# Six-layer stack: the inverse norms of a sequence move from VectorE to GpSimd

## The chip, the cores and the metric

One NeuronCore of a Trainium2 chip runs the whole program. Its engines, as the profile names them, are PE (TensorE, matmuls, with its weight loads as PEld), DVE (VectorE), ACT (ScalarE), POOL (GpSimd) and SP (SyncE, which only issues transfers here). The metric is the device time of one execution in microseconds, median of the runs shown, lower is better.

## The reference, cut to what matters

Four stages run one after the other on 16 sequences of 256 tokens of 128 features: a linear attention, a mixture of experts, a causal linear attention, and then a stack of six layers, each a local attention and a feed-forward. The stack takes most of the time, and the change lies in its attention:

```
qkv = x @ Wqkv;  q, k, v = split(qkv)            # 16 heads of 64
l2norm(t) = t / max(norm(t, axis=-1), 1e-12)
q = l2norm(q) * q_scale;  k = l2norm(k) * k_scale
q = q*cos*scale + rotate_half(q)*sin*scale        # k with 1/scale
out = softmax(mask(8 * q k^T over two windows of 32)) v
x = out @ Wo + x
x = feed_forward(layernorm(shifted x)) + x
```

The norms are those of 64 numbers each: for one sequence 2 tiles of 128 tokens, query and key, 16 heads, so 64 sums of squares in each of 128 partitions. Of each the kernel needs the inverse square root of max(sum, 1e-24).

## The kernel before, in words

A tile is 128 tokens. A sequence has two tiles (TPS), two sequences make a unit, and eight units go through each layer, so the stack has 96 sequences in all. For each of them the code makes a number of *steps*, each a short run of instructions on one engine.

For each tile and for query and key in turn, `projections` makes: on PE the product with the weights into a PSUM buffer "pair" (L1071, two matmuls of 512 columns); on ACT the squares of the product (`square`, L1092); on DVE the two rotary products, `first` (L1078, with the cosines, into a buffer "t1") and `second` (L1085, the swapped halves with the sines, into "t2"), and `squares` (L1098), which sums the squares of each head into "ss"; on POOL `rotated` (L1095), the sum t1 + t2.

When the four sums of a sequence are there, `rotations` makes the step `norms`, which calls `inv_norm`: on DVE one reduction of pairs (L1049, where the second entry of each pair in "ss" was filled with 1e-24 once, so that the reduction is the clamp), a first guess made from the bits of the number with a tile "magic" (L1050), and three Newton rounds of three instructions (L1054, L1055, L1056). These eleven instructions work on 128 x 64 elements. Then `turned` makes, four times in a sequence: on POOL `scale` (L1141), which multiplies t1 by the inverse norms; on PE eight transposes (L1145); on ACT a copy to "qT" or "kT" (L1151).

The rest of a sequence: `windows` (PE L1196, ACT L1187 and L1202); `attention` for each tile with scores (PE L1228), the mask and the maximum (DVE L1236, L1250), the subtraction (POOL L1253), exp (ACT L1257), the total and its reciprocal (DVE L1261, L1262), the division (POOL L1265), transposes (PE L1269), a copy (ACT L1310), the mix with the values (PE L1280) and a copy (ACT L1289); `output` (PE L1340, 32 matmuls, DVE L1349). For each unit a feed-forward follows (PE L1366, L242, L1401, L1421; DVE, ACT, and on POOL a variance's root, L1381 and L221).

The order of the work is set while the program is built, by the class `Plan`. It plays the steps through with an assumed duration for each (the number behind the engine's name in `step(...)`), takes on each engine the ready step of lowest rank for which the buffers are free, and writes the instructions in that order. A rank is the tile's number, plus an entry of the dictionary `due`, plus an entry of the dictionary given to `Plan`, which is looked up by the names of the enclosing function and of the step's function. A lower rank is taken earlier. On the chip each engine then runs its instructions in that fixed order and waits by semaphores for what other engines give it. The buffers that tie the steps together are few: four "pair", five "t1" (a sequence holds four of them, from the product until the transposes have read them), three "ss", two "t2", two "e". `norms` is a DVE step of assumed duration 4.4, `scale` a POOL step of 1.87, `rotated` one of 2.32.

Of the kernel before, what the change touches and what calls it, by code (L numbers as in the profile page):

```python
# [9 lines left out]
F32 = mybir.dt.float32  # L10
I32 = mybir.dt.int32
AF = mybir.ActivationFunctionType
ALU = mybir.AluOpType
AX = mybir.AxisListType
PSUM = bass.MemoryType.PSUM

P = 128
NSEQ = 16
SEQ = 256
TPS = SEQ // P  # L20
# [5 lines left out]
HEADS = 16  # L26
# [37 lines left out]
class Plan:  # L64
# [14 lines left out]
    def step(self, eng, work, fn, after=(), takes=(), uses=(), rank=0, table=None, count=0):  # L79
        after = [a for a in after if a is not None]  # L80
        kind = getattr(fn, "func", fn).__qualname__.split(".<locals>.")[-2:]
        rank += self.due.get(".".join(kind), 0)
        s = Step(eng, work, fn, after, takes, uses, rank, table, count)
        self.steps.append(s)
        return s
# [107 lines left out]
def tile_kernel(ctx: ExitStack, tc: tile.TileContext, a: dict, out: bass.AP):  # L193
    nc = tc.nc
    pe, act, dve, pool, sp = nc.tensor, nc.scalar, nc.vector, nc.gpsimd, nc.sync
# [145 lines left out]
    with ExitStack() as st:  # L341
# [5 lines left out]
        def several(pl, n, shape, name):  # L347
            return [pl.tile(shape, F32, name=f"{name}{k}", tag=f"{name}{k}") for k in range(n)]

        slots = {  # L350
            "bank": several(pa, 6, [P, 512], "pb"),
            "two": several(pa, 1, [P, 2, 512], "pw"),
            "xin": several(wa, 2, [P, TPU, P], "a_xin"),
            "a": several(wa, 8, [P, 512], "a_b"),
            "h": several(wa, 4, [P, 384], "b_h"),
            "x": several(wa, 5, [P, 512], "bc_x"),
            "e": several(wa, 4, [P, 8, 2, DH], "c_e"),
            "va": several(wa, 3, [P, TPS, 8, DH + 1], "c_va"),
# [29 lines left out]
        due = {  # L388
            "linear": -12, "experts": -5, "causal": 0, "hidden": 0, "outer": 0, "values": 0,
            "product": -1, "ends": -1, "turn": 0, "scores": 0, "diagonal": -1, "weigh": 0,  # L390
            "ratio": -1, "y": 0, "join": 0,
        }
        step = plan.step
# [587 lines left out]
    with ExitStack() as st:  # L981
        wps = [wp, st.enter_context(tc.tile_pool(name="wp2", bufs=1))]
        wps = [wp, st.enter_context(tc.tile_pool(name="wp2", bufs=1))]
        cd = st.enter_context(tc.tile_pool(name="cd", bufs=1))
        sd = st.enter_context(tc.tile_pool(name="sd", bufs=3))
        pp = st.enter_context(tc.tile_pool(name="pp", bufs=1, space=PSUM))

        def several(pl, n, shape, name):
# [7 lines left out]
            "xw": several(cd, 2, [P, TPS * NB, P], "d_xw"),  # L996
            "sq": several(cd, 2, hs, "d_sq"),
            "t1": several(cd, 5, hs, "d_t1"),
            "ss": several(cd, 3, [P, 2, 2, HEADS, 2], "d_ss"),
            "t2": several(cd, 2, hs, "d_t2"),  # L1000
            "e": several(cd, 2, [P, 8, 2, 2 * WIN], "d_e"),
            "eT": several(cd, 2, [P, 8, P], "d_eT"),
# [4 lines left out]
        }  # L1007
        for kT in slots["kT"]:
            pool.memset(kT[:, :, 0:WIN], 0.0)
        for ss in slots["ss"]:  # L1010

            pool.memset(ss, 1e-24)
        plan = Plan(slots, {
            "projections.product": -3,
            "feed_forward.turn": 1.5,
            "attention.mix": -1.5,
            "attention.divide": -0.5,
            "output.product": 2,
            "attention.below": 5,
            "projections.first": -0.5,  # L1020
            "projections.squares": 0.5,
            "projections.second": -1,
            "final.turn_back": -3,
            "windows.turn": -1,
            "rotations.norms": 3,
        })

        due = {
# [4 lines left out]
        step = plan.step  # L1033

        def heads(ap):
            return ap.rearrange("p (h d) -> p h d", d=DH)
# [3 lines left out]
            return ap.rearrange("p (h x d) -> p h x d", x=2, d=DH // 2)[:, :, ::-1, :]  # L1040

        NN = TPS * 2 * HEADS
        magic = cd.tile([P, NN], I32, name="d_magic")
        pool.memset(magic, 1597463007)

        def inv_norm(ss):

            x, y, t = (sd.tile([P, NN], F32, name=f"d_n{k}", bufs=2) for k in "xyt")
            dve.tensor_reduce(x, ss.rearrange("p t g h b -> p (t g h) b"), AX.X, ALU.max)  # L1049
            dve.scalar_tensor_tensor(  # L1050
                y.bitcast(I32), x.bitcast(I32), -0.5, magic, ALU.mult, ALU.add
            )
            for _ in range(3):
                dve.scalar_tensor_tensor(t, y, 1.0, y, ALU.mult, ALU.mult)  # L1054
                dve.scalar_tensor_tensor(t, t, -0.5, x, ALU.mult, ALU.mult)  # L1055
                dve.scalar_tensor_tensor(y, t, 1.5, y, ALU.add, ALU.mult)  # L1056
            return y

        def projections(q, t):

            rank = q.rank + t
            xj = q.x[:, WIN + t * P : WIN + (t + 1) * P]
            o = Part()
            o.t1s, o.adds = [], []
            if t == 0:
                q.ss, q.reds = Buf("ss"), []

            def product(qk, pj):
                for hf in range(2):
                    c = qk * INNER + hf * 512  # L1070
                    pe.matmul(  # L1071
                        pj.t[:, hf * 512 : (hf + 1) * 512], lhsT=xj,
                        rhs=q.w["qkv"][:, c : c + 512], start=True, stop=True,
                    )

            def first(qk, pj, t1):
                cc = slice(qk * DH, (qk + 1) * DH)
                dve.tensor_tensor(  # L1078
                    t1.t, heads(pj.t), bc(q.lay.tab[:, 0, t, cc], hs, 1), ALU.mult
                )  # L1080

            def second(qk, pj, t2):
                cc = slice(qk * DH, (qk + 1) * DH)
                h4 = [P, HEADS, 2, DH // 2]
                dve.tensor_tensor(  # L1085
                    t2.t.rearrange("p h (x d) -> p h x d", x=2), swapped(pj.t),
                    bc(q.lay.tab[:, 1, t, cc].rearrange("p (x d) -> p x d", x=2), h4, 1),
                    ALU.mult,
                )

            def square(pj, sq):
                act.activation(sq.t, heads(pj.t), AF.Square)  # L1092

            def rotated(t1, t2):
                pool.tensor_tensor(t1.t, t1.t, t2.t, ALU.add)  # L1095

            def squares(qk, sq):
                dve.tensor_reduce(q.ss.t[:, t, qk, :, 0], sq.t, AX.X, ALU.add)  # L1098

            for qk in range(2):  # L1100
                pj, sq, t1, t2 = Buf("pair"), Buf("sq"), Buf("t1"), Buf("t2")
                mm = step(
                    "pe", 1.82, partial(product, qk, pj), [*q.ready, *q.loaded, q.gate(t)],
                    [pj, t1], rank=rank + due["project"], count=8,
                )
                s = step(
                    "act", 0.92,
                    partial(square, pj, sq),
                    [mm], [sq], [pj], rank,
                )  # L1110
                a1 = step("dve", 1.13, partial(first, qk, pj, t1), [mm, q.tabbed], [], [pj, t1], rank)
                a2 = step(
                    "dve", 1.13, partial(second, qk, pj, t2), [mm, q.tabbed], [t2], [pj],
                    rank + due["second"],
                )
                new = [] if q.reds else [q.ss]
                q.reds.append(
                    step(
                        "dve", 1.13, partial(squares, qk, sq), [s, *q.reds], new,
                        [sq] if new else [sq, q.ss], rank + due["squares"],  # L1120
                    )
                )
                o.adds.append(
                    step(
                        "pool", 2.32,
                        partial(rotated, t1, t2),
                        [a1, a2], [], [t1, t2], rank,
                    )
                )
                o.t1s.append(t1)  # L1130
            q.tiles.append(o)

        def rotations(q):


            def norms():
                q.rn = inv_norm(q.ss.t)

            def scale(t, qk, t1):
                k = (2 * t + qk) * HEADS  # L1140
                pool.tensor_tensor(t1.t, t1.t, bc(q.rn[:, k : k + HEADS], hs, 2), ALU.mult)  # L1141

            def turn(t1, pz):
                for c in range(8):
                    pe.transpose(  # L1145
                        pz.t[:, c * P : (c + 1) * P],
                        t1.t[:, 2 * c : 2 * c + 2, :].rearrange("p h d -> p (h d)"), ident,
                    )

            def put(dst, off, pz):  # L1150
                act.copy(  # L1151
                    dst.t[:, :, off : off + P], pz.t.rearrange("p (c n) -> p c n", n=P)
                )

            nm = step("dve", 4.4, norms, q.reds, [], [q.ss], q.rank + due["norms"])
            q.kT = Buf("kT")
            for t in range(TPS):
                turned(q, t, nm, scale, turn, put)
# [318 lines left out]
        for i in range(DEPTH):  # L1477
# [22 lines left out]
            for u in range(NU):  # L1500
                adds = []
                for s in range(SPU):
                    q = Seq()
# [171 lines left out]
```

## Time and profile before

| what | value |
|---|---|
| runs shown | 4375.12, 4375.44, 4377.77 us; median 4375.44 |
| the profiled execution: time, span from first to last instruction | 4371.72 us, 4369.9 us |
| mean granted TensorE clock | 0.989 |
| DVE busy in the span | 3633.8 us (83%) |
| ACT busy in the span | 2674.8 us (61%) |
| POOL busy in the span | 2978.6 us (68%) |
| first and last Newton product on DVE (L1056) | 1116.7 and 4268.2 us from the start |

The first three stages fill the span up to about 1095 us; the stack follows. The table of groups of instructions gives, for each line of the code, engine and shape, the count, the busy time, the mean duration of one, the idle time of the engine just before these instructions, and what released it. The table of waits tells who waited for whom. The timeline lists an engine's instructions in order of time, neighbours of one kind merged ("x4"). A PE that is busy need not be at its peak, since the ends of matmuls are modelled. Durations on POOL are rougher than on DVE and ACT.

### The profile page before, as it was taken

How to read it: one execution, taken by the hardware profiler on the slowest of the kernel's cores; microseconds unless marked ns; L12 is line 12 of the kernel's file. 1: busy time of each engine (PE TensorE's matmuls, PEld its weight loads, DVE VectorE, ACT ScalarE, POOL GpSimd, SP SyncE). 2: the span in 40 equal slices, each digit the busy share in tenths (PEclk: the TensorE clock that was granted, in tenths of full speed). 3: DMA queues.
4: the chain of work that ended last, by engine and by line, in shares of the span. 5: the costliest groups of instructions: out<-in, count | busy, mean ns of one | idle time of the engine just before them, and what ended most of it. 6: DMA issues, size and time to landing. Idle time of an engine off the chain costs nothing. (4 is left out here: it accounts for less than half of the span.)

```text
span 4369.9 us, 106120 instructions
## 1 busy us (share of the span) xinstructions
PE 4191.8 (96%) x45648; PEld 2978.9 (68%) x45648; DVE 3633.8 (83%) x6064; ACT 2674.8 (61%) x3514; POOL 2978.6 (68%) x1717
## 2 busy tenths in 40 slices
PE   8999999998699999999999999999999999999998
PEld 6777877877466666666666666666666666666666
DVE  6888888877788888878888888888888878888895
ACT  6766767664466566566656656666665665665654
POOL 2655545555787777767777778777777777777773
PEclk9999999999899999999999999999999999999999
DMA  3000000000000000000000000000000000000000
GB/s 88 4 6 6 3 4 1 4 3 3 20 2 11 2 13 2 7 11 2 13 2 6 11 2 13 2 7 11 2 12 2 7 11 2 2 2 6 6 14 18
DMA packets 30834, 37.13 MB, mean 8 GB/s; under 512 B 5407, under 2 KB 24349, under 8 KB 29597
## 3 DMA queue, kind: packets, MB, share of 16 engines
q1 hardware_dynamic: 30364, 30.35, 2.3%
q8 instruction: 359, 5.88, 0.6%
q14 instruction: 111, 0.90, 0.1%
HBM read 26.15 MB, written 4.19 MB: 7 GB/s over the span
## 5 line engine op out<-in xcount | busy, mean ns | idle before, releaser
L1095 POOL TENSOR_TENSOR d_t<-d_t,d_t 128x1024 f32<-128x1024 f32 x384 | 906.3, 2366 | 301.7 <-DVE d_t L1078 230.7
L1141 POOL TENSOR_TENSOR d_t<-d_t,d_ny 128x1024 f32<-128x1024 f32 x384 | 718.8, 1902 | 242.3 <-DVE d_ny L1056 242.3
L1071 PE MATMUL pp<-d_wqkv,xs 128*128 128x512 f32 x1536 | 736.7, 605 | 6.5 <-ACT d_sq L1092 1.6
L1340 PE MATMUL pp<-d_zT,d_wvo 128*128 128x256 f32 x3072 | 687.5, 382 | 1.2 <-DVE d_t L1078 0.5
L1340 PEld LDWEIGHTS pp<-d_zT,d_wvo 128*128 128x128 f32 x3072 | 575.9, 190 | 85.0 <-ACT d_xw L1202 1.3
L1092 ACT ACTIVATE d_sq<-pp 128x1024 f32<-128x1024 f32 x384 | 393.4, 1024 | 313.8 <-PE pp L1071 174.4
L1085 DVE TENSOR_TENSOR d_t<-pp,d_tab 128x1024 f32<-128x1024 f32 x384 | 466.3, 1215 | 135.4 <-ACT d_sq L1092 94.5
L1265 POOL TENSOR_TENSOR d_e<-d_e,d_z 128x1024 f32<-128x1024 f32 x192 | 363.5, 1902 | 229.6 <-DVE d_z L1262 228.3
L1289 ACT COPY d_zT<-pp 128x1024 f32<-128x1024 f32 x384 | 384.1, 1016 | 192.6 <-PE pp L1280 190.3
L1078 DVE TENSOR_TENSOR d_t<-pp,d_tab 128x1024 f32<-128x1024 f32 x384 | 463.7, 1209 | 19.0 <-ACT d_sq L1092 19.0
L1228 PEld LDWEIGHTS pp<-d_kT,d_qT 64*32 64x32 f32 x24576 | 230.2, 106 | 352.9 <-issue 202.1
L1098 DVE TENSOR_REDUCE d_ss<-d_sq 128x16 f32<-128x1024 f32 x384 | 463.3, 1209 | 0.1
L1280 PE MATMUL pp<-d_eT,d_xw 64*128 64x256 f32 x3072 | 425.9, 402 | 21.7 <-DVE d_t L1078 12.7
L1145 PE MATMUL pp<-ident,d_t 128*128 128x128 f32 x3072 | 404.2, 278 | 35.5 <-POOL d_t L1141 24.0
L1071 PEld LDWEIGHTS pp<-d_wqkv,xs 128*128 128x128 f32 x1536 | 271.4, 191 | 241.5 <-issue 217.2
L1145 PEld LDWEIGHTS pp<-ident,d_t 128*128 128x128 f32 x3072 | 344.8, 142 | 104.6 <-issue 56.4
L1257 ACT ACTIVATE d_e<-d_e 128x1024 f32<-128x1024 f32 x192 | 202.8, 1057 | 317.4 <-POOL d_e L1253 312.7
L1228 PE MATMUL pp<-d_kT,d_qT 64*32 64x64 f32 x24576 | 348.7, 223 | 28.7 <-DVE d_t L1078 25.0
L1253 POOL TENSOR_TENSOR d_e<-d_e,d_m 128x1024 f32<-128x1024 f32 x192 | 363.7, 1903 | 16.7 <-DVE d_m L1250 16.7
L848 POOL TENSOR_TENSOR c_e<-c_e,c_sm 128x1024 f32<-128x1024 f32 x128 | 248.7, 1950 | 178.2 <-DVE c_sm L844 121.8
L1280 PEld LDWEIGHTS pp<-d_eT,d_xw 64*128 64x128 f32 x3072 | 270.7, 187 | 104.0 <-ACT d_eT L1310 28.3
L835 POOL TENSOR_TENSOR c_e<-c_mn,c_e 128x512 f32<-128x512 f32 x128 | 139.7, 1091 | 196.3 <-ACT c_e L825 95.7
(187 smaller groups left out, 8083.1 us busy)
## 6 DMA issues: line engine op xcount, KB each, us to landing
d_wqkv<-L_ffn_Wqkv SPq DMA_DIRECT2D x6, 1024.0 KB
d_t<-L_ffn_Wqkv SPq DMA_DIRECT2D x10, 256.0 KB
d_t<-L_ffn_Wo SPq DMA_DIRECT2D x10, 256.0 KB, 3.0
a_xin<-L_attn_x SPq DMA_DIRECT2D x8, 256.0 KB, 2.9
keep<-bc_x SPq DMA_DIRECT2D x8, 256.0 KB, 2.0
d_t<-keep SPq DMA_DIRECT2D x8, 256.0 KB, 3.0
out<-d_t SPq DMA_DIRECT2D x8, 256.0 KB, 2.4
d_w<-L_ffn_W SPq DMA_DIRECT2D x6, 341.0 KB
```

Source lines behind the costliest of these rows:

```text
L1071: pe.matmul(pj.t[:, hf * 512 : (hf + 1) * 512], lhsT=xj, rhs=q.w["qkv"][:, c : c + 512], start=True, stop=True,)
L1078: dve.tensor_tensor(t1.t, heads(pj.t), bc(q.lay.tab[:, 0, t, cc], hs, 1), ALU.mult)
L1085: dve.tensor_tensor(t2.t.rearrange("p h (x d) -> p h x d", x=2), swapped(pj.t), bc(q.lay.tab[:, 1, t, cc].rearrange("p (x d) -> p x d", x= ...
L1092: act.activation(sq.t, heads(pj.t), AF.Square)
L1095: pool.tensor_tensor(t1.t, t1.t, t2.t, ALU.add)
L1098: dve.tensor_reduce(q.ss.t[:, t, qk, :, 0], sq.t, AX.X, ALU.add)
L1141: pool.tensor_tensor(t1.t, t1.t, bc(q.rn[:, k : k + HEADS], hs, 2), ALU.mult)
L1145: pe.transpose(pz.t[:, c * P : (c + 1) * P], t1.t[:, 2 * c : 2 * c + 2, :].rearrange("p h d -> p (h d)"), ident,)
L1228: pe.matmul(pS.t[b * WIN : (b + 1) * WIN, s0 : s0 + 2 * WIN], lhsT=qT.t[r, c, b * WIN : (b + 1) * WIN], rhs=kT.t[r, c, k0 : k0 + 2 * WIN], ...
L1280: pe.matmul(pz.t[:, par * 512 : (par + 1) * 512].rearrange("p (c n) -> p c n", n=QB)[:, :, j * WIN : (j + 1) * WIN], lhsT=q.xw.t[r, t * NB ...
L1289: act.copy(q.zT.t[:, 2 * t + g, :, :].rearrange("p h n -> p (h n)"), pz.t)
L1340: pe.matmul(pr.t[:, :SEQ], lhsT=q.w["vo"][:, h, :], rhs=q.zT.t[:, :, h, :], start=(h == 0), stop=(h == HEADS - 1),)
```

## The change

`inv_norm` is written for POOL and called from a POOL step of assumed duration 2.8. It clamps the sums in place, makes the first guess with the magic number as an immediate, and takes four instructions for a Newton round, since none of them has two tensors and a scalar. DVE keeps `squares`, which now writes a plain "ss". The fills of "ss" and the tile "magic" go, and two small buffers get three copies each in place of three buffers with two. The planner's second dictionary is rewritten: seven entries have other numbers, five are new.

```diff
-            "ss": several(cd, 3, [P, 2, 2, HEADS, 2], "d_ss"),
+            "ss": several(cd, 3, [P, TPS, 2, HEADS], "d_ss"),
...
-        for ss in slots["ss"]:
-
-            pool.memset(ss, 1e-24)
         plan = Plan(slots, {
-            "projections.product": -3,
+            "projections.product": -1,
             "feed_forward.turn": 1.5,
-            "attention.mix": -1.5,
+            "attention.mix": -4.5,
             "attention.divide": -0.5,
-            "output.product": 2,
-            "attention.below": 5,
-            "projections.first": -0.5,
-            "projections.squares": 0.5,
-            "projections.second": -1,
+            "output.product": 4,
+            "attention.below": 3,
+            "projections.first": -1.5,
+            "projections.squares": -1.0,
+            "projections.second": 3,
             "final.turn_back": -3,
             "windows.turn": -1,
             "rotations.norms": 3,
+            "join.turn": -3,
+            "join.turned_out": 4,
+            "rotations.turn": -0.5,
+            "attention.top": -1.5,
+            "rotations.put": -3,
         })
...
-        magic = cd.tile([P, NN], I32, name="d_magic")
-        pool.memset(magic, 1597463007)
-
-        def inv_norm(ss):
-
-            x, y, t = (sd.tile([P, NN], F32, name=f"d_n{k}", bufs=2) for k in "xyt")
-            dve.tensor_reduce(x, ss.rearrange("p t g h b -> p (t g h) b"), AX.X, ALU.max)
-            dve.scalar_tensor_tensor(
-                y.bitcast(I32), x.bitcast(I32), -0.5, magic, ALU.mult, ALU.add
+
+        def inv_norm(x):
+
+            y, t = (sd.tile([P, NN], F32, name=f"d_n{k}", bufs=3) for k in "yt")
+            pool.tensor_scalar(x, x, 1e-24, None, ALU.max)
+            pool.tensor_scalar(
+                y.bitcast(I32), x.bitcast(I32), -0.5, 1597463007.0, ALU.mult, ALU.add
             )
             for _ in range(3):
-                dve.scalar_tensor_tensor(t, y, 1.0, y, ALU.mult, ALU.mult)
-                dve.scalar_tensor_tensor(t, t, -0.5, x, ALU.mult, ALU.mult)
-                dve.scalar_tensor_tensor(y, t, 1.5, y, ALU.add, ALU.mult)
+                pool.tensor_tensor(t, y, y, ALU.mult)
+                pool.tensor_tensor(t, t, x, ALU.mult)
+                pool.tensor_scalar(t, t, -0.5, 1.5, ALU.mult, ALU.add)
+                pool.tensor_tensor(y, y, t, ALU.mult)
             return y
...
-                dve.tensor_reduce(q.ss.t[:, t, qk, :, 0], sq.t, AX.X, ALU.add)
+                dve.tensor_reduce(q.ss.t[:, t, qk, :], sq.t, AX.X, ALU.add)
...
-                q.rn = inv_norm(q.ss.t)
+                q.rn = inv_norm(q.ss.t.rearrange("p t g h -> p (t g h)"))
...
-            nm = step("dve", 4.4, norms, q.reds, [], [q.ss], q.rank + due["norms"])
+            nm = step("pool", 2.8, norms, q.reds, [], [q.ss], q.rank + due["norms"])
```

## The prediction

> **What bounds the kernel now.** I read the stack in equal windows first, then the waits of PE, then the timelines of one sequence. In the windows of the inner layers the columns are the stretch, its length, and the busy time with the count for PE, PEld, DVE, ACT and POOL, then the clock.
>
> ```profile
> 1500.00:2100.00 600.00, 591.84 (x7423) 401.51 (x7420) 513.78 (x752) 370.33 (x386) 454.84 (x239) 1.00 0.02 6
> 2100.00:2700.00 600.00, 592.12 (x7375) 400.35 (x7373) 513.56 (x751) 370.34 (x385) 455.20 (x239) 1.00 0.03 8
> ```
>
> PE is busy for 98.6% of such a stretch, DVE for 85.6%, POOL for 75.8%, at full clock. PE's ends are modelled, but the timeline below shows its runs set end to end with no gap, so PE's order sets the pace. PE does nothing less after the change: a gain can only come out of its idle time, or of shorter idle at the edges of layers.
>
> The groups of the steps in question, from the table of groups by shape (count | busy us, mean ns | idle before, releaser):
>
> ```profile
> L1141 POOL TENSOR_TENSOR d_t<-d_t,d_ny 128x1024 f32<-128x1024 f32 x384 | 718.8, 1902 | 242.3 <-DVE d_ny L1056 242.3
> ...
> L1050 DVE SCALAR_TENSOR_TENSOR d_ny<-d_nx,d_magic 128x64 int32<-128x64 int32 x96 | 104.1, 1085 | 3.3
> ...
> L1054 DVE SCALAR_TENSOR_TENSOR d_nt<-d_ny 128x64 f32<-128x64 f32 x288 | 72.2, 251 | 9.9
> ```
>
> POOL stands idle 242.3 us, 2.5 us a sequence, for DVE's inverse norms, and has nothing else to do then. L1050 takes 1085 ns where its like, L1056, takes 225: something holds it up. Now one sequence on POOL, on DVE and on PE (start, length, engine, line):
>
> ```profile
> 1625.45 1.90 POOL L1253 TENSOR_TENSOR d_e<-d_e,d_m 128x1024 f32<-128x1024 f32 x1
> 1629.85 7.48 POOL L1141 TENSOR_TENSOR d_t<-d_t,d_ny 128x1024 f32<-128x1024 f32 x4 [2.50 <-DVE d_ny L1056]
> 1637.30 1.89 POOL L1265 TENSOR_TENSOR d_e<-d_e,d_z 128x1024 f32<-128x1024 f32 x1
> ```
>
> ```profile
> 1624.03 1.21 DVE L1098 TENSOR_REDUCE d_ss<-d_sq 128x16 f32<-128x1024 f32 x1
> 1625.28 0.29 DVE L1049 TENSOR_REDUCE d_nx<-d_ss 128x64 f32<-128x128 f32 x1
> 1625.60 1.83 DVE L1050 SCALAR_TENSOR_TENSOR d_ny<-d_nx,d_magic 128x64 int32<-128x64 int32 x1
> ```
>
> ```profile
> 1633.13 0.45 PE L1228 MATMUL pp<-d_kT,d_qT 64*32 64x64 f32 x32
> 1633.51 1.99 PE L1145 MATMUL pp<-ident,d_t 128*128 128x128 f32 x16
> 1635.34 1.88 PE L1071 MATMUL pp<-d_wqkv,xs 128*128 128x512 f32 x4
> ```
>
> The last sum of squares ends at 1624.03 + 1.21 = 1625.24, the first scale (L1141) starts at 1629.85: 4.6 us. L1050 ends at 1627.43, just behind POOL's L1253 at 1627.35: it had waited for it. The first scale ends at 1631.7, and PE turns that tile at 1633.51, 1.8 us later; the second ends at 1633.6 and is turned at about 1634.4, **0.8 us** later. In the other sequence of the unit the scales start at 1663.33 and PE's first turn is at 1671.35, 6.1 us behind the first scale's end. So half of the sequences are tight.
>
> **What DVE loses.** L1049, L1050, L1054, L1055 and L1056: 27.3 + 104.1 + 72.2 + 64.9 + 64.9 = 333.4 us busy, with 2.8 + 3.3 + 3 x 9.9 = 35.8 us of gaps between them, 369 us in all, 3.85 us a sequence. DVE isn't the bound, so this counts only where PE waits for DVE. In the table of PE's waits the DVE rows of the stack are 25.0 (L1228), 12.7 (L1280), 6.0 (L1145), 5.3 (L1280) and 5.1 (L1269): 54 us is the most that a freer DVE can give. I take half, **-27 us**, because those waits sit behind products, not behind norms, and the order is new anyway. The 242 us of POOL's idle time are no gain by themselves: PE didn't wait there.
>
> **What POOL gains in work.** Fourteen instructions on 128 x 64, each using the one before it. No such row exists. The nearest are POOL's root, in the timeline:
>
> ```profile
> 1653.41 0.24 POOL L1381 TENSOR_SCALAR f_rs<-f_mv 128x4 f32<-128x4 f32 x1
> 1653.74 1.04 POOL L221 TENSOR_TENSOR f_rs<-f_rs,nhalf 128x4 f32<-128x4 f32 x1
> ```
>
> The second needs the first's result and starts 0.32 to 0.33 us after it: 0.24 of work and 0.085 of gap. Independent ones have no gap: four L1141 of 1.902 start 1.87 apart. For 64 elements in place of 4, the fills show the slope for one operand: 151 ns for 64 elements, 204 for 128, so 0.83 ns an element, and a scalar instruction takes 232 + 60 x 0.83 = 282 ns, 0.365 us with the gap. For two full tensors L1095 has 2366 ns at 1024 elements; with 232 fixed that is 2.08 ns an element, 365 ns at 64, 0.45 with the gap. Nine of these and five scalar ones: 9 x 0.45 + 5 x 0.365 = **5.9 us**. Lower end: all at the small row's 0.315, 4.4 us. Upper end: a fixed part of 352 ns, from the table rows L1463 (726 ns at 256) and L835 (1091 at 512), 7.0 us, and the integer guess as dear as L221's power adds 0.7: 7.7. I take 5.9, since the root is the nearest row in size and in dependence.
>
> Two rules bear on this. The Trainium skill, "Perfetto Trace Analysis", section GPSIMD Engine Instruction, says that spans of this engine are unreliable and that one should time from start to start. By spans alone the sum is 9 x 0.365 + 5 x 0.282 = 4.7; by starts, 5.9. The two rows above decide for starts, because the gap of 0.085 is visible. "GPSIMD Engine Reference", section Engine selection, speaks against the move: elementwise work belongs on VectorE, GpSimd being about twice as slow for two inputs. By it 14 x 2 x 0.225 = 6.3 us, an estimate that puts the step no cheaper than mine. The planner's 2.8 lies under all of these, even under the lower end.
>
> Per sequence (96 in 4268.2 - 1116.7 us, so 33.2 us each) POOL has 0.758 x 33.2 = 25.2 us of work. With 5.9 it has 31.1: 94% full.
>
> **What comes late.** With the old order POOL would start the norms at 1627.35, when L1253 is done, and the first scale at 1633.25 in place of 1629.85; in the other sequence the squares end at 1659.35, POOL is busy until 1660.83, and the scale starts at 1666.7 in place of 1663.33. Both are 3.4 us late. With the planner's 2.8 the same sum is 0.3. So the new order is made for scales that in truth arrive 3.1 us later. Behind the norms on POOL stand the four scales, then a division (L1265) or a subtraction (L1253): exp and the transposes of e come late too, with larger margins on PE. Where a turn has 0.8 us of margin in the plan, PE stands for 2.3 us, and every engine behind it.
>
> I assume that the new order has margins as the old one: one tight sequence in two. Of the 48 units the first and last of a layer run irregularly (joins, tables), so about 42 count: 42 x 2.3 = **+97 us**. In the fill at 1100 to 1200 us POOL is the late engine already (L1145 waits for L1141 three times, 24.0 us); there the norms take 5.9 for DVE's 4.0 us, **+6 us**.
>
> **The smaller edits**, together: fills of ss and magic (0.65 us before the stack, hidden by DVE's start) and the third copy of y and t, nothing; `squares` writes 16 numbers with a narrower stride, nothing. The new ranks move work that has the same length: DVE's second product now comes behind the first, the squares nearer to them, the mix earlier on PE, products and output later. No DMA is added. The order can be worth anything between the idle time that PE has in the stack, 117 us from the windows (length less PE busy, from 1100 us on), and as much lost; I set nothing for it beyond the -27.
>
> Sum against the profiled execution: 4371.7 + 97 + 6 - 27 = 4447.7. The median shown is 3.7 above that execution: **4450 us**.
>
> **Rivals.**
> - *PE hides it.* The new order leaves every turn over 3 us of margin, as the slack sequence has (6.1), and DVE's waits go: -27 to -54 us, some 4335. For it: POOL still has 2 us a sequence free, L1050's hold-up (0.86 us x 96 on DVE) disappears, and squares now run earlier. Against it: 94% on POOL with a fixed order. Chance 0.29. This is the case on the other side; it decides where the true step is under about 3.6 us, 2.8 plus the tight margin, or where the margins are wide.
> - *Gain and cost cancel* within 0.2% (9 us, about what a measurement of this kernel tells from no change). Chance 0.12.
> - *POOL becomes the bound* in every sequence. Its other waits before were 3.1 us (L1095) and 2.4 us (L1265) a sequence; if two thirds stay, 31.1 + 3.7 = 34.8 against 33.2, 96 x 1.6 = 154 us, 4530; if all stay, 4720. For it: `t1` has five buffers, so the next products wait for the late turns. Against it: a late POOL finds its operands ready. Chance 0.17.
> - *The step costs 2.8* after all: then it is the first rival with less wait; it is in its chance.
>
> The likeliest, one tight turn per unit, has 0.42, with its own range 4390 to 4500 (the step from 4.4 to 7.7 gives 4385 to 4526). Faster 0.29, same 0.12, slower 0.59. From 4335 to 4550 leaves out the best fifth of the first rival and the worse half of POOL as the bound.
>
> **What will show it.** In the changed profile: the 14 POOL instructions start to start (5.9 a sequence); POOL near 94% of the inner windows, DVE near 75%; PE's first wait for POOL L1141 at L1145 in the inner layers, about 2 us each time; PE under 97% of an inner window. It is wrong if POOL's norms take under 4 us, or if PE stays at 98.6% with POOL's scales late, which would mean wide margins.

## The result, and the profile after

| | median, us | runs |
|---|---|---|
| before | 4375.73 | 4 |
| changed | 4693.80 | 4 |

The ratio is 1.0725, 95% interval 1.0707 to 1.0744: the change costs **318 us**. The direction was forecast, the size was not: 4450 was predicted, and 4693.8 lies above the range.

The windows of the inner layers of the changed kernel (stretch, length, busy time with count of PE, PEld, DVE, ACT, POOL, clock):

```profile
1500.00:2100.00 600.00, 557.61 (x6681) 364.13 (x6682) 404.86 (x496) 329.69 (x345) 472.89 (x437) 0.98 0.02 6
2100.00:2700.00 600.00, 555.93 (x6570) 363.41 (x6570) 403.23 (x504) 326.66 (x342) 478.84 (x454) 0.99 0.02 6
```

PE went from 592 us busy to 557 in 600, and every engine but POOL does less in the same stretch. POOL is busy for 79%, so no engine is full: each of them waits for another. Over the whole span PE does the same 45,648 matmuls in both kernels. It is idle for 363 us in place of 178, and busy for 4326 us in place of 4192. So 185 us of the loss are waits of PE, and 134 us are matmuls that take longer. Of these the granted clock (0.980 in place of 0.989 on average) accounts for at most 46 us, an estimate from 0.020 x 4689 less 0.011 x 4370. The norms on POOL, one sequence, from the timeline of the changed kernel:

```profile
2032.28 0.38 POOL L1049 TENSOR_SCALAR d_ss<-d_ss 128x64 f32<-128x64 f32 x1
2032.74 0.24 POOL L1050 TENSOR_SCALAR d_ny<-d_ss 128x64 int32<-128x64 int32 x1
2033.07 0.29 POOL L1054 TENSOR_TENSOR d_nt<-d_ny 128x64 f32<-128x64 f32 x1
2033.44 0.32 POOL L1055 TENSOR_TENSOR d_nt<-d_nt,d_ss 128x64 f32<-128x64 f32 x1
...
2037.46 2.37 POOL L1096 TENSOR_TENSOR d_t<-d_t,d_t 128x1024 f32<-128x1024 f32 x1
```

From 2032.28 to 2037.46 are **5.2 us**, with the gap of 0.08 us behind each instruction. The planner has 2.8 for it. Next the table of waits of PE in that kernel (engine, tile, line, released by; us, times, longest):

```profile
PE pp L1270 <- DVE d_t L1086: 62.2, 43, 1.7
PE pp L1146 <- POOL d_t L1142: 50.0, 20, 15.6
PE pp L242 <- DVE f_xc L1387: 47.8, 33, 1.5
PE pp L1402 <- DVE d_t L1086: 23.5, 34, 1.0
```

The wait that I had named, turns (L1146) for scales (L1142), is there, but with 50 us in the whole run, the fill included. More of it hangs on DVE: on `second` (L1086), whose end frees a "pair" buffer, and on the feed-forward's centring (L1387). DVE itself had been freed of the norms, and yet it is late. The centring is late because of POOL, as DVE's own table of waits shows:

```profile
DVE f_xc L1387 <- POOL f_rs L221: 175.4, 43, 4.8
```

It waits for the variance's root (L221), which mostly stands behind the norms in POOL's queue; the section on lateness comes back to it. For `second` it is another matter. The group of `first`, which stands ahead of it on DVE, in the changed kernel and in the one before shows what DVE waits for (count | busy, mean ns | idle before it, releasers):

```profile
L1079 DVE TENSOR_TENSOR d_t<-pp,d_tab 128x1024 f32<-128x1024 f32 x384 | 465.1, 1212 | 630.9 <-ACT d_sq L1093 491.4
```

```profile
L1078 DVE TENSOR_TENSOR d_t<-pp,d_tab 128x1024 f32<-128x1024 f32 x384 | 463.7, 1209 | 19.0 <-ACT d_sq L1092 19.0
```

DVE waited 19 us for ACT's square at this line before (and 94.5 at L1085, which then came first), and 491 after. In the program `first` doesn't use the square; it reads the same product. One instance from the changed kernel's timelines, ACT and then DVE:

```profile
2047.91 1.02 ACT L1093 ACTIVATE d_sq<-pp 128x1024 f32<-128x1024 f32 x1 [1.29 <-PE pp L1072]
```

```profile
2049.03 1.23 DVE L1079 TENSOR_TENSOR d_t<-pp,d_tab 128x1024 f32<-128x1024 f32 x1 [9.44 <-ACT d_sq L1093]
```

The square ends at 2048.93 and DVE starts 0.1 us later. Paired in order and compared by start and end, none of the 384 squares overlaps its `first` or its `second`, in either kernel: the two engines read a PSUM buffer one after the other. The Trainium skill states the reason, in "PSUM — Partial Sum Buffer", section PSUM bank collisions raise a hardware error: ScalarE and VectorE must not access one bank in one partition at once, reads against reads included, so software orders them. The planner doesn't know this: in `projections` the square and both rotary products have the product alone as predecessor.

So there were two candidates behind the 318 us: a step that takes 5.2 us where the order was made for 2.8, and new ranks that run into these holds ("held reads" below), which the plan doesn't count.

### The profile page after: what moved, and what is told of

It is laid out like the page before. It is cut to its first block, busy times and chain, and to the rows that moved or that the text cites. A ratio compares the mean times of both kernels' runs of the same rounds, so it can differ in the third digit from the quotient of the medians.

```text
span 4689.4 us, 106172 instructions
## 1 busy us (share of the span) xinstructions
PE 4326.1 (92%) x45648; PEld 2992.1 (64%) x45648; DVE 3301.6 (70%) x5008; ACT 2666.5 (57%) x3516; POOL 3376.0 (72%) x3057
## 4 chain that ended last, share of the span: by engine, by line
POOL 22%; PE 20%; DVE 16%; ACT 9%; issue 6%; POOLq 0%; ACTq 0%; DVEq 0%
PE pp L1072 7%; DVE d_t L1079 6%; POOL d_t L1142 5%; ACT d_sq L1093 5%; DVE d_t L1086 4%; POOL d_t L1096 4%; POOL d_e L1254 3%; PE pp L1341 2%; PE pp L1146 2%; DVE d_e L1237 2%; POOL d_nt L1055 2%; PE pp L1281 2%; POOL d_ny L1057 2%; DVE d_ss L1099 2%; POOL d_nt L1054 2%
## 5 line engine op out<-in xcount | busy, mean ns | idle before, releaser
L1072 PE MATMUL pp<-d_wqkv,xs 128*128 128x512 f32 x1536 | 766.9, 630 | 26.7 <-ACT d_eT L1311 10.8
L1142 POOL TENSOR_TENSOR d_t<-d_t,d_ny 128x1024 f32<-128x1024 f32 x384 | 718.1, 1901 | 0.5
L1086 DVE TENSOR_TENSOR d_t<-pp,d_tab 128x1024 f32<-128x1024 f32 x384 | 464.3, 1210 | 53.3 <-ACT d_sq L1093 51.7
L1072 PEld LDWEIGHTS pp<-d_wqkv,xs 128*128 128x128 f32 x1536 | 281.7, 198 | 315.3 <-issue 255.1
L1146 PE MATMUL pp<-ident,d_t 128*128 128x128 f32 x3072 | 414.7, 282 | 62.2 <-POOL d_t L1142 50.0
L1281 PE MATMUL pp<-d_eT,d_xw 64*128 64x256 f32 x3072 | 413.8, 400 | 5.2 <-DVE d_e L1237 2.5
L1146 PEld LDWEIGHTS pp<-ident,d_t 128*128 128x128 f32 x3072 | 337.8, 143 | 126.5 <-POOL d_t L1142 57.2
L1402 PE MATMUL pp<-f_xn,d_w 128*128 128x512 f32 (+1 forms) x576 | 315.5, 635 | 29.7 <-DVE d_t L1086 23.5
L1396 ACT ACTIVATE f_xn<-pp,d_bias 128x512 f32<-128x512 f32 x48 | 37.3, 778 | 451.1 <-PE pp L242 451.1
```

The lines of the kernel that those rows point to most:

```text
L1072: pe.matmul(pj.t[:, hf * 512 : (hf + 1) * 512], lhsT=xj, rhs=q.w["qkv"][:, c : c + 512], start=True, stop=True,)
L1086: dve.tensor_tensor(t2.t.rearrange("p h (x d) -> p h x d", x=2), swapped(pj.t), bc(q.lay.tab[:, 1, t, cc].rearrange("p (x d) -> p x d", x= ...
L1146: pe.transpose(pz.t[:, c * P : (c + 1) * P], t1.t[:, 2 * c : 2 * c + 2, :].rearrange("p h d -> p (h d)"), ident,)
L1281: pe.matmul(pz.t[:, par * 512 : (par + 1) * 512].rearrange("p (c n) -> p c n", n=QB)[:, :, j * WIN : (j + 1) * WIN], lhsT=q.xw.t[r, t * NB ...
```

## The experiments

Each kernel stands beside the kernel before on the same chip, whose median was 4374.5 to 4377.6 us. Ratios have their 95% interval.

### The two parts of the change apart, and the true duration

```diff
# ranks_alone: the kernel before, with the changed kernel's ranks
-            "projections.product": -3,
+            "projections.product": -1,
...
# move_alone: the changed kernel, with the ranks of before
# after_5_2: the changed kernel
-            nm = step("pool", 2.8, norms, q.reds, [], [q.ss], q.rank + due["norms"])
+            nm = step("pool", 5.2, norms, q.reds, [], [q.ss], q.rank + due["norms"])
# move_5_2: the same line, with the ranks of before
# old_plan_on_pool: ranks of before, POOL's instructions
+            nm = step("dve", 4.4, norms, q.reds, [], [q.ss], q.rank + due["norms"])
```

> The kernel before (norms on DVE, assumed 4.4) with the twelve plus five ranks of the changed kernel. Late-step theory (the time comes from POOL's norms taking 5.2 us where the planner assumes 2.8): within 1% of before, 4330 to 4420. Rank theory (the new ranks give PE an order that waits wherever the norms run): most of the 318 us is here, 4600 to 4750. Joint theory (the ranks only hurt together with the POOL step): 4380 to 4450.

> The changed kernel with the ranks of before: the norms run on POOL and the planner assumes 2.8 for them. Late-step theory: most of the slowdown is here, 4550 to 4700. Rank theory: 4370 to 4450, since PE keeps an order close to the old one. Joint theory: in between, 4450 to 4550.

> The changed kernel with the planner's duration of the norms set from 2.8 to the 5.2 us measured; nothing else is edited. Late-step theory: the plan now knows of the lateness, so the waits of PE for POOL go and the time falls to 4400 to 4480. Rank theory: still above 4600.

> The norms on POOL with the ranks of before and the planner told 5.2. Late-step theory: the lateness is gone, what is left is the order's fit: 4420 to 4480, under the 4638 of the same ranks with 2.8. Rank theory: about the same as with 2.8.

> The order of before on PE, DVE and ACT is kept (the planner still treats the norms as a DVE step of 4.4 us), but the norms' 14 instructions are issued on POOL at that point of the order. By the prediction's own sum, with 5.2 in place of 5.9 us: scales come 2.7 us later in the tight sequence of each unit, margin 0.8, so about 1.9 us x 48 = 90 us, 4440 to 4490. If PE hides it: 4330 to 4380. If POOL becomes the bound at its 5.2 us more a sequence: over 4550.

| kernel | us | ratio to before | planner's own length of the stack |
|---|---|---|---|
| before | 4375 | 1 | 3255 |
| changed | 4693.8 | 1.0725 (1.0707 to 1.0744) | 3259 |
| ranks_alone | 4554.9 | 1.0405 (1.0389 to 1.0421) | 3329 |
| move_alone | 4638.2 | 1.0596 (1.0580 to 1.0612) | 3271 |
| after_5_2 | 4555.4 | 1.0406 (1.0391 to 1.0422) | 3358 |
| move_5_2 | 4606.7 | 1.0529 (1.0513 to 1.0544) | 3310 |
| old_plan_on_pool | 4640.4 | 1.0600 (1.0582 to 1.0617) | 3255 |

The last column is what the class `Plan` adds up from its assumed durations while the program is built; it is no time of the chip. Neither the late-step theory nor the rank theory holds alone: each part by itself costs four to six per cent, and they don't add. ranks_alone and after_5_2 lie between the ranges set for them, and move_5_2 is only 31 us under move_alone. The plan thought the changed kernel as long as the one before. Telling it the true 5.2 took 138 us off on the chip, with ranks that weren't made for that.

old_plan_on_pool is the sharpest against my prediction. It has the old order on PE, so its margins are the ones I had read, and my sum gives 90 us; it lost 263. Its timelines on POOL, ACT and PE:

```profile
1743.31 0.36 POOL L1044 TENSOR_SCALAR d_ss<-d_ss 128x64 f32<-128x64 f32 x1
...
1748.48 1.90 POOL L1249 TENSOR_TENSOR d_e<-d_e,d_m 128x1024 f32<-128x1024 f32 x1
1750.34 7.48 POOL L1137 TENSOR_TENSOR d_t<-d_t,d_ny 128x1024 f32<-128x1024 f32 x4
```

```profile
1750.41 1.06 ACT L1253 ACTIVATE d_e<-d_e 128x1024 f32<-128x1024 f32 x1 [11.99 <-POOL d_e L1249]
1751.38 1.00 ACT L1088 ACTIVATE d_sq<-pp 128x1024 f32<-128x1024 f32 x1
1752.28 1.92 ACT L1285 COPY d_zT<-pp 128x1024 f32<-128x1024 f32 x2
```

```profile
1749.40 0.45 PE L1224 MATMUL pp<-d_kT,d_qT 64*32 64x64 f32 x32
1753.43 1.94 PE L1265 MATMUL pp<-ident,d_e 128*128 128x128 f32 x8 [3.57 <-ACT d_zT L1285]
1755.90 3.37 PE L1141 MATMUL pp<-ident,d_t 128*128 128x128 f32 x16
```

In this order the norms stand ahead of a subtraction (L1249), which starts 5.2 us later for it. The prediction had put them behind that subtraction, so this isn't quite the order that it priced; but move_alone, where the planner itself places the step on POOL, lost 261 us. ACT's exp takes that result with no margin (it ends at 1750.38, exp starts at 1750.41), and ACT's queue is held behind exp: a square and two copies of finished "pair" buffers. PE wants one of these buffers and stands 3.57 us. The stall isn't all: the eight transposes behind it take 1.94 us where the same shape took 1.09 before. The windows of that kernel around it say why:

```profile
1745.00:1749.00 4.00, 4.00 (x82) 2.28 (x82) 0.74 (x2) 0.00 (x0) 3.26 (x11) 1.00 0.02 4
1749.00:1753.00 4.00, 0.85 (x38) 0.36 (x34) 0.52 (x1) 2.59 (x3) 4.00 (x3) 0.87 0.00 0
1753.00:1757.00 4.00, 3.57 (x45) 3.10 (x46) 3.96 (x5) 2.21 (x3) 4.00 (x3) 0.50 0.00 0
1757.00:1761.00 4.00, 4.00 (x25) 2.76 (x31) 2.58 (x3) 2.02 (x2) 4.00 (x3) 0.77 0.02 4
```

The granted clock, the third number from the end, is 0.50 after the stall. The waits of PE for L1285 sum to 136.7 us in 40 times, and the mean clock is 0.959 against 0.989. Over the span PE is idle for 158 us more than before, and busy for 112 us more with the same matmuls; the two make up the loss.

### How much is lateness

```diff
# after_one_round (and after_two_rounds with 2), order untouched
-            for _ in range(3):
+            for _ in range(1):
                 pool.tensor_tensor(t, y, y, ALU.mult)
# before_one_round: the same in the kernel before
-            for _ in range(3):
+            for _ in range(1):
                 dve.scalar_tensor_tensor(t, y, 1.0, y, ALU.mult, ALU.mult)
```

> The changed kernel, order and ranks untouched, with two of the three Newton rounds left out: the step on POOL then has 6 instructions, about 2.2 us, under the 2.8 that the plan assumes. Late-step theory (the slowdown is that the step takes 5.2 where the order was made for 2.8): 4370 to 4410. Rank theory (the new order loses by itself, as with the norms on DVE): about 4500 or more. Mixed: 4410 to 4480.

> The same with one round left out: 10 instructions, about 3.7 us, 0.9 over the plan. Late-step theory with a margin of about 1 us in the plan: within 30 us of the one-round kernel. If every us of lateness costs the same: a third to two thirds of the way from the one-round kernel to the changed one at 4694.

> The kernel before with two of three Newton rounds left out on DVE, order untouched: DVE has 1.5 us less to do a sequence (6 instructions less at about 0.257 from start to start). If DVE's time is worth nothing, as the PE at 98.6% says: 4355 to 4380. If freeing DVE gains what the change hoped for: under 4340.

One round: 4534.8 us, 1.0357 (1.0338 to 1.0376). Two rounds: 4575.5, 1.0458 (1.0442 to 1.0473). From about 2.2 to 3.7 us of step the kernel loses 41 us, which fits neither theory of the margin (under 30, or a third of the way and more), and from 3.7 to 5.2 another 118. So the first microsecond beyond the plan is mostly absorbed, and what comes after it is not: lateness makes 159 us of the 318. The rest, 160, is there although the step ends before the plan's time. Leaving out rounds also takes up to 3 us of work a sequence off POOL; pool_retuned_2 below, with all 14 instructions, shows that this work as such can be hidden.

The traces show where the lateness reaches PE. One unit of the changed kernel, on POOL, DVE and PE; the last norm (L1057) ends at 2178.73:

```profile
2178.81 0.23 POOL L1382 TENSOR_SCALAR f_rs<-f_mv 128x4 f32<-128x4 f32 x1
2180.20 1.37 DVE L1387 TENSOR_SCALAR f_xc<-pp,f_mv,f_rs 128x128 f32<-128x128 f32 x4 [4.81 <-POOL f_rs L221]
2180.76 1.20 PE L242 MATMUL pp<-ident,f_xc 128*128 128x128 f32 x4 [1.45 <-DVE f_xc L1387]
```

In 37 of the 48 units the feed-forward's root stands right behind the norms in POOL's queue. DVE's centring, and everything behind it on DVE, waits for the root. With one round the same waits are 1.8 us in place of 4.8:

```profile
DVE f_xc L1387 <- POOL f_rs L221: 64.8, 40, 1.8
```

PE's waits for the centring go from 47.8 us to 0.2 with two rounds and 0 with one, which is part of why the last microseconds of the step are the dear ones. PE's waits for scales (L1146) go from 50.0 to 17.5. In all PE is idle for 101 us less with one round, and busy for 56 us less.

before_one_round: 4357.8, 0.9961 (0.9946 to 0.9976). Taking 1.5 us of small instructions a sequence off DVE is worth 17 us. Freeing DVE isn't worth nothing, but it is small.

### What makes the other half

```diff
# after_no_bank, one_round_no_bank (also with range(1)), before_no_bank
             def square(pj, sq):
-                act.activation(sq.t, heads(pj.t), AF.Square)
+                act.activation(sq.t, heads(q.w["qkv"][:, :INNER]), AF.Square)
```

> The changed kernel, order untouched, but the square on ACT reads 1024 numbers of the weights in SBUF instead of the product in PSUM (so the sums and norms are those of other numbers). ACT does the same work; the square and the two rotary products on DVE no longer read one PSUM buffer. Held-reads theory (the planner lets DVE and ACT read a buffer at once, the chip lets them do so one after the other, and the new ranks put DVE's read right behind the product): 4500 to 4570, since the lateness of the norms stays. If those holds are covered: within 30 us of 4694.

> Both taken away from the changed kernel, its order untouched: one Newton round (about 2.2 us, under the plan's 2.8) and the square from SBUF. Held-reads theory: the planner's picture is then true, and its lengths of the stack are 3259 here and 3255 before, so 4365 to 4410. Rival (PE runs this order more slowly whatever arrives when: short runs, switches between shapes): still 4500 or more, as with one round alone (4535).

> The control: the kernel before with the square from SBUF, norms on DVE. If its order covers the holds: 4350 to 4380. If the removed read helps any order, by freeing ACT earlier: under 4330, and the two kernels above must be read against that.

| kernel | us | ratio to before |
|---|---|---|
| after_no_bank | 4524.6 | 1.0341 (1.0325 to 1.0356) |
| one_round_no_bank | 4327.7 | 0.9890 (0.9875 to 0.9905) |
| before_no_bank | 4307.5 | 0.9843 (0.9826 to 0.9859) |

The control moved by 68 us, as its second expectation had it: even the old order pays for the shared reads. Against it, the changed order with one round pays 207. With both things taken away the changed order is within 20 us of the old one without the shared reads. one_round_no_bank lies under its range because that had left out what the old order pays. The windows of before_no_bank and of one_round_no_bank:

```profile
1500.00:2100.00 600.00, 600.00 (x7490) 408.58 (x7488) 520.58 (x774) 370.42 (x391) 464.06 (x244) 1.00 0.03 8
1500.00:2100.00 600.00, 599.29 (x7371) 400.16 (x7369) 449.53 (x552) 366.20 (x387) 486.26 (x346) 1.00 0.03 8
```

PE is busy for 599 of 600 us with the changed order. So the rival of slow runs on PE can't explain the 318 us. It may have a part in the last 20: over the span PE is busy for 4219 us here and for 4186 in before_no_bank, with the same matmuls, while it is idle for 16 us less.

On PE the held reads show as waits for "pair" buffers that `second` frees late. The transposes of the attention (L1270) have the largest, in after_one_round and then in one_round_no_bank:

```profile
L1270 PE MATMUL pp<-ident,d_e 128*128 128x128 f32 x1536 | 206.0, 277 | 80.9 <-DVE d_t L1086 62.8 <-ACT d_zT L1290 17.5 <-POOL d_e L1266 0.2
L1270 PE MATMUL pp<-ident,d_e 128*128 128x128 f32 x1536 | 204.7, 276 | 0.4
```

The group of `first` in that kernel has lost its wait for ACT:

```profile
L1079 DVE TENSOR_TENSOR d_t<-pp,d_tab 128x1024 f32<-128x1024 f32 x384 | 464.4, 1210 | 408.1 <-PE pp L1072 401.6 <-ACT d_kT L1152 4.3 <-ACT d_eT L1311 1.1
```

It now waits for PE's product, as the plan has it. DVE's own idle time is no measure of the cost: it goes over from ACT to PE here, and pool_retuned_2 below waits 256 us for the square and is fast. What counts is that PE stops waiting. The account of the 318 us by these medians: lateness 4693.8 - 4534.8 = **159**; shared reads 207.1 - 68.1 = **139**; left over 4327.7 - 4307.5 = **20**. Taken in the other order, with the reads removed first, they are 169 - 68 = 101 for the reads and 4524.6 - 4327.7 = 197 for the lateness: the two overlap by some 40 us, and both stay large. The edit also lets the square start without PE's product, so a part of the reads' share may be ACT's freedom; the control has the same freedom, and the difference is what I use.

### Can an order hide the step

In these the ranks are searched anew: many sets are played through with the assumed durations, and the shortest is taken. The first two know the 5.2. The last two are also told of the shared reads, in the plan and in the search.

```diff
# pool_retuned_1, pool_retuned_2, pool_told_1
-            nm = step("pool", 2.8, norms, q.reds, [], [q.ss], q.rank + due["norms"])
+            nm = step("pool", 5.2, norms, q.reds, [], [q.ss], q.rank + due["norms"])
# pool_told_1, dve_told_1: both rotary products
-                a1 = step("dve", 1.13, partial(first, qk, pj, t1), [mm, q.tabbed], [], [pj, t1], rank)
+                a1 = step("dve", 1.13, partial(first, qk, pj, t1), [mm, s, q.tabbed], [], [pj, t1], rank)
```

> The norms on POOL, the planner told 5.2, and the ranks searched anew so that the planner's own length of the stack is 3245 us (before: 3255; changed kernel with 5.2: 3358). If a POOL step of 5.2 us can be hidden by an order made for it: 4360 to 4420. If POOL at 31 us of work in 33 can't keep up on the chip: over 4480.

> The same with another set of ranks from the search, planner's length 3248 us. Same expectations; that two orders of equal length in the plan agree within 1% on the chip would say that the plan's length carries over.

> The kernel before, norms on DVE, where the planner is told that the two rotary products start only after the square (both get it as a predecessor), and the ranks are searched anew with the holds counted. If what the planner doesn't know is worth time in the kernel before too: 4300 to 4360. If PE is at its limit there: 4360 to 4390.

> The norms on POOL, the planner told both things it lacked (5.2 us for the norms, the rotary products behind the square), ranks searched anew by the same search as for dve_told_1. If the place of the norms matters little once the plan is right: 4340 to 4390. If POOL's fuller queue costs at any order: over 4400.

| kernel | norms on | us | ratio to before |
|---|---|---|---|
| pool_retuned_1 | POOL | 4421.8 | 1.0106 (1.0091 to 1.0121) |
| pool_retuned_2 | POOL | 4381.2 | 1.0011 (1.0001 to 1.0021) |
| pool_told_1 | POOL | 4388.0 | 1.0024 (1.0014 to 1.0034) |
| dve_told_1 | DVE | 4349.2 | 0.9939 (0.9924 to 0.9954) |

The norms on POOL can be hidden: pool_retuned_2 has the same steps as the changed kernel, in another order, and runs 313 us faster. Its window:

```profile
1500.00:2100.00 600.00, 595.25 (x7339) 397.60 (x7335) 451.82 (x549) 363.65 (x382) 524.30 (x489) 1.00 0.02 6
```

POOL is at 87%, and PE at 99%. So POOL's fuller queue isn't a bound here. pool_retuned_1 misses the range of 4360 to 4420 by 2 us. That both retuned kernels would agree within 1% was just met (0.9%, 41 us), with the plan's lengths 3245 and 3248 in the wrong order: the plan's length ranks orders that lie close no better than that.

No order with the norms on POOL beat the kernel before: under a plan that knows both things, POOL gives 4388 and DVE 4349. These 39 us don't show that DVE is the better place, since two orders of the same steps on POOL lie 41 us apart. dve_told_1 beats the kernel before by 26 us; how much of that comes from the ranks and how much from the holds that its planner knows isn't shown. Its ranks:

```
"projections.product": -6, "attention.mix": -2, "attention.divide": 3.5, "output.product": 2,
"attention.below": -8, "projections.first": -1, "projections.squares": 3, "projections.second": -8,
"final.turn_back": -8, "windows.turn": -7.5, "rotations.norms": -7.5, "feed_forward.outer": -8,
"attention.mask": 0.5, "projections.square": -4.5, "attention.put": -4, "attention.scores": -5.5,
"windows.spread": -4.5, "join.turned_out": -8, "attention.exps": -7.5, "attention.top": -1,
"feed_forward.gated": -8, "attention.put_e": -7, "feed_forward.stats": -5, "projections.rotated": 3,
"output.add": -8, "rotations.put": 3, "attention.total": -5, "join.turn": -8,
"windows.put": -4, "rotations.scale": -5.5, "feed_forward.inner": 2,
```

## Why the prediction was wrong

Its own steps, in turn.

- **What bounds the kernel: PE** - right for the kernel before (before_no_bank reaches PE busy in the whole window), and right that what can be won is PE's idle time: of the 68 us that the shared reads cost there, 57 were idle time of PE.
- **DVE's relief, -27** - of the right size: 17 us for 1.5 of the 3.85 us a sequence, in the old order.
- **The step on POOL, 5.9 us** - 5.2 measured, inside the ends. Starting to starting was the right way: the durations of the 14 alone are 397 us in 96 sequences, 4.1 us. I was high because a small instruction with two tensors takes 0.29 to 0.32 us and not 0.365. That the planner's 2.8 is too low was right. Two readings were off without weight: the rows L1463 and L835 give a fixed part of 361 ns, not 352, and the +6 for the fill took 4.0 us for DVE's norms, which take 2.9 there (from 1115.68, the end of the sums, to the first scale at 1118.62).
- **The price of the lateness, +97** - this step failed. It said: "I assume that the new order has margins as the old one: one tight sequence in two", and that exp and the transposes come late "with larger margins on PE". Only the turns of scaled tiles were priced. With the old order on PE (old_plan_on_pool) the loss was 263 us, through subtraction, exp, ACT's queue and a "pair" buffer, with PE's halved clock on top. In the changed order it was 159, and the largest wait of PE that goes with it lies on a path that the prediction doesn't have: norms, the feed-forward's root, DVE's centring, PE. The turns' waits in the inner layers were 11.7 us in nine times (1500 to 3900 us), where +97 was set. I had the exp row before me, which starts 0.04 us behind L1253 (2026.85 and 2026.81) after 6.65 us of waiting, and read it as harmless since ACT is busy for 61% only. ACT's queue has other work behind exp, and that work frees PE's buffers.
- **The new ranks, nothing** - this term failed as well. It was set to zero because no work is added, and the prediction allowed that "the order can be worth anything" without putting it into the range. It is worth about 139 us (101 by the other way), because the new order has `first`, and with it `second`, wait for ACT's read of the same product, which the plan doesn't see.
- **The rivals** - PE hiding it didn't happen with these ranks, though pool_retuned_2 shows that it can. POOL as the bound was wrong as a cause: it is at 79%, and at 87% in the fast pool_retuned_2. That its dearest case, 4720, lies 26 us from the measured time is luck.
- **What would show it** - PE under 97% of an inner window: 92.8%. POOL near 94%, DVE near 75%: 79% and 67%, since the whole became slower. About 2 us for each first turn: seen in places (1.96 us at 2041.74), but 50 us in all. PE's busy time, for which the prediction has no term, rose by 134 us.

What is left open: the last 20 us between the two orders, how the reads' share divides between the held reads and ACT's earlier start, and why PE's matmuls take longer in the changed kernel beyond the 46 us of clock. The surplus shrinks to 33 us when lateness and shared reads are gone, so most of it comes with the stalls.

## What to carry to other kernels

When a kernel's order comes from a planner, a moved step is priced by the planner's number: hold that number against the trace first, and treat changed ranks as a change of its own, with its own run. Follow a late step through every queue in which other work stands behind it, not only to the consumer that it was made for; here it was queues of engines with much idle time, POOL's and ACT's, whose order hurt. And let the planner know all that orders instructions on the chip, here two engines that read one PSUM buffer: an order that looked equally long in the plan cost three per cent more for it.

## What the runs showed of the hardware

- PE's granted clock fell to 0.50 behind a stall of 3.57 us, and eight transposes took 1.94 us in place of 1.09. By the two rows with 0.50 and 0.77 the stall cost some 2.7 us of PE's time in clock on top (an estimate: half of 3.57 and 0.23 of 4.00). "TensorE: Matmul & The Clock Gate" of the Trainium skill, section What's actually happening, gives an idle window of about 3.4 us for the fall. In the changed kernel less was enough: stalls of 1.96 and 0.77 us, ended at 2041.74 and 2043.60 with eight transposes between them, were followed by a clock of 0.69 from 2044 to 2048.
- A POOL instruction of 128 x 64 that uses the one before it takes 0.24 us for one tensor, 0.29 to 0.32 for two, and 0.08 of gap; the clamp at the head takes 0.37. It is 5.2 us for 14. The eleven on DVE took 3.2 us from the start of the first to the first scale where L1050 took 0.43 us (1660.15 to 1663.33), and 4.6 where it took 1.83 beside POOL's L1253 (1625.28 to 1629.85).
